# A graph layer on one core: node loads moved to GpSimd's queue, other dst blocks, a split last pair

## The chip, the core and the metric

The kernel runs on one NeuronCore of a Trainium2 chip. A core has five engines that each work through their own instruction stream: TensorE (PE, matrix multiply), VectorE (DVE), ScalarE (ACT), GpSimd (POOL) and SyncE (SP, which only issues transfers here). The metric is the device time in microseconds of one execution. The kernel before was run three times: 355.16, 357.14 and 358.20 us, so its median is 357.14 us.

## The reference, cut to what matters

There are 12,500 nodes with 128 features, and 412,500 edges with 48 features. The list `dst` names the node that each edge ends at. The inputs are sorted by it.

```python
h   = relu(layernorm(x))                                # per node, 128 features
agg = segment_sum(edge_attr, dst, num_segments=12500)   # per node, 48 features
u   = graph_globals[0]                                  # 64 numbers, the same for all nodes
hid = relu(concat([h, agg, u]) @ W1 + b1)               # 240 -> 256
out = x + hid @ W2 + b2                                 # 256 -> 128
```

Everything is float32. The edges are 79.2 MB; x and out are 6.4 MB each.

## The kernel before, in words

**Two streams of edges.** The edge list is cut into two halves, stream 0 and stream 1, which are worked in step. An edge chunk is 1024 edges, laid out as 128 partitions with 8 edges each. Six chunks of one stream make a group, and there are 34 groups per stream (`NI`). One step of the main loop (`for step in range(CG * NI + 3)`, L677) takes chunk number k of group i from both streams; I call it a k-step, and there are about 201 of them.

**The segment sum as a matrix product.** The destinations of a group fall in a narrow window of nodes. VectorE builds a one-hot matrix that says for each edge which column of the window it belongs to (`onehot`, L325 to L342: three instructions per group, for the chunk pairs 0 and 2 together and 1 alone, once the loop runs). TensorE multiplies the edges' features with it and sums in PSUM (`contract`, L344 to L357, tile `ps`). When a group is done, VectorE adds the window to the sums in SBUF at a column read from a register (`add`, L359 to L367, tile `aggT`).

**What the one-hot needs.** The list `first` holds one middle edge's dst per group, from which the window's place is taken. `dst` itself is loaded in blocks of several groups (`begins`, L79; `load_dst`, L189): a block has one row of 1024 numbers per chunk. `shift_dst` (L388) subtracts the window's place (two small matmuls, a copy, one ScalarE pass), `spread` (L400) turns the rows with eight transposes and ScalarE copies (tile `rel`), `check_dst` (L422) makes two ScalarE passes over a block that look for edges outside the window. If there were any, a slow general path would run at the end; here it doesn't.

**The node part.** Nodes are worked in pairs of blocks, one from each stream's range: 512 + 512 nodes, twelve pairs, and last a middle block of 212. For each pair: load x (`load_x`, L204; L214), statistics per row on VectorE (`bn_stats`, L491), the normalised rows on ScalarE (`xn`, L487), transposes on TensorE and a ScalarE copy out of PSUM (`transpose`, L498; tile `hT`), the first layer from x (`hidden_x`, L511; tile `ph`), the first layer from the sums (`hidden_sums`, L528), relu on ScalarE (tile `hid`), the second layer (`output`, L547; tile `po`), and an addition of x + b2 with the store (`store`, L560).

**What sets the order.** Each engine's order is fixed when the program is built. The main loop issues a k-step of `contract`, then what `plan` has for that step (loads, shifts, spreads and checks of dst blocks at fixed steps before a block begins), then at every third step an x load that is due (`next_x`), the adds and one-hots, one or two parts of the normalisation (`next_part`), and then pieces of the node part for which a credit suffices (0.72 us per step, at most 1.2; the pieces cost 0.45 or 0.9). A pair's sums may begin when the groups below its nodes are added (`ready`, L115). What is left after the last step is worked off at the end.

**Transfers.** SP issues `first`, the edge tiles (`load_edges`, L144, two chunks or 384 KB in each, 15 buffers) and the later dst blocks, and the stores. ACT's queue carries dst block 0 and all x loads, so these stand among ScalarE's compute instructions. GpSimd issues the weights once, at the start, after its constants. Transfers take one of eight completion counters in turn; the loads issued from SP and from ACT share one set of eight, those from GpSimd have another. A load that takes a counter again first waits until the counter's previous transfer has landed. The engine whose queue holds the load stops there.

**At the start**, SP issues `first` (three loads), five edge tiles, the two halves of dst block 1 (54 rows each), then the other edge tiles. ACT issues the two halves of dst block 0 (24 rows each). The blocks are 4, 9, 9, 9 and 3 groups long.

Of the kernel before, what the change touches and what calls it, by code (L numbers as in the profile page):

```python
# [9 lines left out]
F32 = mybir.dt.float32  # L10
I32 = mybir.dt.int32
AF = mybir.ActivationFunctionType
OP = mybir.AluOpType
# [3 lines left out]
P = 128  # L17
# [4 lines left out]
def kernel(  # L22
# [30 lines left out]
    nc = tc.nc  # L53
# [24 lines left out]

    begins = [0] + list(range(4, NI, 9)) + [NI]  # L79
    NB = len(begins) - 1  # L80
# [4 lines left out]
    R = 4  # L85
# [7 lines left out]

    NP = N // BN // 2
    MID = NP * BN
    NM = N - 2 * NP * BN
    END = MID + NM
    assert NM % R == 0 and NM < BN
    blocks = []
    for k in range(NP):  # L100
        blocks += [(k * BN, P), (END + k * BN, P)]
    blocks.append((MID, NM // R))
    pairs = [[2 * k, 2 * k + 1] for k in range(NP)] + [[2 * NP]]

# [10 lines left out]
    ready = [min(NI - 1, max(  # L115
        int(-(-(blocks[j][0] + BN + PAD + 1 - LEAST - BEGIN[s]) // GSTEP)) - 1
        for s, j in enumerate(pairs[k]))) for k in range(NP)]
# [78 lines left out]

    def rows_of(ap, a, m):

        return ap[a:a + m * R].rearrange("(p r) d -> p (r d)", p=m)

# [3 lines left out]
    def load_x(k):  # L204

        if k >= len(pairs):
            return
        xt = xp.tile([P, 2, R * D], F32, name="xt")
        xts[k] = xt

        def load(i, j):
            a, m = blocks[j]
            f = m - m % 16
            nc.scalar.dma_start(xt[:f, i], rows_of(x, a, f))  # L214
            if f < m:
                nc.scalar.dma_start(xt[f:m, i], rows_of(x, a + f * R, m - f))

        for i, j in enumerate(pairs[k]):
            xs[j] = xt[:, i].rearrange("p (r d) -> p r d", d=D)
            x_loads.append((k, lambda i=i, j=j: load(i, j), step))  # L220
# [19 lines left out]
    with nc.allow_non_contiguous_dma(reason="a few hundred numbers, once"):  # L240
        for s in range(2):
            mid0 = C0[s] * CE
            n = min(NI, (E - mid0) // GE)
            nc.sync.dma_start(
                first[:, s * NI:s * NI + n],
                dst[mid0:mid0 + n * GE].rearrange("(a g e) -> a g e", a=1, e=GE)[:, :, GE // 2])
            for i in range(n, NI):
                m = mid0 + i * GE + GE // 2
                assert m < E
                nc.sync.dma_start(first[:, s * NI + i:s * NI + i + 1], dst[None, m:m + 1])  # L250
    dis = {0: load_dst(0, nc.scalar)}
    for i in range(PF):
        next_edges()
        if i == 4:
            dis[1] = load_dst(1, nc.sync)

# [28 lines left out]
    eps = const.tile([P, 1], F32)  # L285
    nc.gpsimd.memset(eps, EPS)
    nc.gpsimd.memset(w1a, 0.0)
    with nc.allow_non_contiguous_dma(reason="a few hundred numbers, once"):
# [7 lines left out]
        nc.gpsimd.dma_start(b2_sb, b2[None, :].to_broadcast([P, D]))  # L296
    for c in range(0, NC, 1024):
        nc.gpsimd.memset(aggT[:, c:min(c + 1024, NC)], 0.0)
# [3 lines left out]
    nc.gpsimd.memset(span, 0.0)  # L302
    step = -4
    for k in range(XBUFS):
        load_x(k)
    warm = const.tile([P, 1], F32)
# [150 lines left out]
    def normalization(k):  # L457

        js = pairs[k]
        m = blocks[js[0]][1]  # L460
        q = len(js) * R
        st = sp.tile([P, 2 * R, 6], F32, name="st", bufs=2)
# [20 lines left out]
        def row(i, j, r):  # L483
            if r == 0:
                xns[j] = mp.tile([P, R, D], F32, name="xn")
            c = i * R + r
            nc.scalar.activation(xns[j][:m, r], xs[j][:m, r], AF.Relu, bias=sh[:m, c:c + 1], scale=sc[:m, c:c + 1])  # L487

        for i, j in enumerate(js):
            for r in range(R):  # L490
                parts.append((k, None, lambda i=i, j=j, r=r: nc.vector.bn_stats(st[:m, i * R + r, :], xs[j][:m, r, :])))  # L491
        parts.append((k, None, variance))
        parts.append((k, None, finish))
        for i, j in enumerate(js):
            for r in range(R):
                parts.append((k, j, lambda i=i, j=j, r=r: row(i, j, r)))

    def transpose(j):  # L498
        m = blocks[j][1]
        pt = pst.tile([P, R, P], F32, name="pt")  # L500
        xn = xns.pop(j)
        for r in range(R):
            nc.tensor.transpose(pt[:, r, :m], xn[:m, r], ident[:m, :m])  # L503

        hT = mp.tile([P, P, R], F32, name="hT", bufs=4)
        nc.scalar.copy(hT[:, :m], pt[:, :, :m].rearrange("d r p -> d p r"))  # L506
        hTs[j] = hT.rearrange("d p r -> d (p r)")

    phs = {}

    def hidden_x(k, a, j):  # L511

        m = blocks[j][1]
        if a == 0:
            hids[j] = mp.tile([P, NH, R, P], F32, name="hid", bufs=4)
            js = pairs[k]
            if j == js[0]:
                xb = mp.tile([P, 2 * R, D], F32, name="xb", bufs=2)
                nc.vector.tensor_tensor(xb[:m, :len(js) * R], xts[k].rearrange("p i (r d) -> p (i r) d", d=D)[:m, :len(js) * R],  # L519
                                        b2_sb[:m, None, :].to_broadcast([m, len(js) * R, D]), OP.add)  # L520
                for n, q in enumerate(js):
                    xbs[q] = xb[:, n * R:(n + 1) * R]
        phs[j, a] = psh.tile([P, BN], F32, name="ph")
        for c in (0, HI):
            nc.tensor.matmul(phs[j, a][c:c + HI, :R * m], w1h[:, a * P + c:a * P + c + HI], hTs[j][:, :R * m],  # L525
                             start=True, stop=False, skip_group_check=True)

    def hidden_sums(k, a):  # L528

        js = pairs[k]  # L530
        if len(js) == 2:
            for s, j in enumerate(js):
                at = blocks[j][0] + shift[s]
                h = slice(s * HI, s * HI + DE)
                for c in (0, HI):
                    nc.tensor.matmul(phs[j, a][c:c + HI], w1a[h, a * P + c:a * P + c + HI], aggT[h, at:at + BN],  # L536
                                     start=False, stop=True, skip_group_check=True)
        else:
            for c in (0, HI):
                nc.tensor.matmul(phs[js[0], a][c:c + HI, :NM], w1a[:K2, a * P + c:a * P + c + HI], mid[:K2],  # L540
                                 start=False, stop=True, skip_group_check=True)
        for j in js:
            m = blocks[j][1]
            nc.scalar.activation(hids[j][:, a, :, :m], phs.pop((j, a))[:, :R * m].rearrange("h (p r) -> h r p", r=R),  # L544
                                 AF.Relu, bias=bias[:, a:a + 1])

    def output(j, r):  # L547

        m = blocks[j][1]
        if r == 0:  # L550
            pos[j] = pso.tile([P, R, D], F32, name="po")
        for a in range(NH):
            for c in range(0, m, HI):
                k = min(m, c + HI)
                nc.tensor.matmul(pos[j][c:k, r], hids[j][:, a, r, c:k], w2[:, a], start=(a == 0), stop=(a == NH - 1),  # L555
                                 skip_group_check=True)
        if r == R - 1:
            late.append(j)

    def store(j):  # L560
        a0, m = blocks[j]
        ot = mp.tile([P, R, D], F32, name="ot")
        nc.vector.tensor_tensor(ot[:m], pos.pop(j)[:m], xbs.pop(j)[:m], OP.add)  # L563
        k = m - m % 16
        od = ot.rearrange("p r d -> p (r d)")
        nc.sync.dma_start(rows_of(out, a0, k), od[:k])
        if k < m:
            nc.sync.dma_start(rows_of(out, a0 + k * R, m - k), od[k:m])

# [13 lines left out]
    for k, js in enumerate(pairs):  # L583
        at = CG * ((ready + [NI - 1])[k] + 1) + 2
        nxt = pairs[k + 2] if k + 2 < len(pairs) else []
        if len(js) == 1:
            pieces.append((at, 0.0, lambda: copy_middle(0)))
        parts_of = [(at - (8 if k else 12), 0.9, lambda k=k, a=a, j=j: hidden_x(k, a, j)) for a in range(NH) for j in js]
        sums = [(at, 0.9, lambda k=k, a=a: hidden_sums(k, a)) for a in range(NH)]
        m = len(js)  # L590
        pieces += parts_of[:m + 1] + (early[2:] if k == 0 else []) + sums[:1] + parts_of[m + 1:] + sums[1:]
        for s in range(2):
            if s < len(nxt):
                pieces.append((at, 0.9, lambda j=nxt[s]: turn(j)))
            if s < len(js):
                for r in range(R):
                    pieces.append((at, 0.45, lambda j=js[s], r=r: output(j, r)))
# [46 lines left out]
    first_nodes(1)  # L644
    next_x()
    next_x()

# [29 lines left out]
    for step in range(CG * NI + 3):  # L677
# [5 lines left out]
        if step % 3 == 2:  # L683
            next_x(4)
        if k == 0:
# [12 lines left out]
        while pieces and pieces[0][0] <= step and pieces[0][1] <= credit:  # L698
            credit -= pieces[0][1]
            pop_piece()  # L700
    step += 99
    while pieces:
# [7 lines left out]
    with tc.If(isbad >= 1):  # L710
# [63 lines left out]
        for k, js in enumerate(pairs):  # L774
# [12 lines left out]
            for j in js:  # L787
                for r in range(R):
                    output(j, r)
                store_late()  # L790
# [28 lines left out]
```

## Time and profile before

| | |
|---|---|
| median of three runs | 357.14 us |
| the profiled execution: its time, and its span in the trace | 362.16 us, 360.3 us |
| TensorE busy | 310.8 us (86%) |
| VectorE, ScalarE, GpSimd busy | 239.6, 112.8, 13.9 us |
| the transfers' mean rate over the span | 265 GB/s |
| idle time of TensorE before 41.87 us | 21.6 us |
| last k-step ends, last matmul ends, span ends | 333.84, 353.06, 360.3 us |
| granted TensorE clock, mean | 0.951 |

The profile is of one execution. Each row of a view gives its start and its length in us from the span's start; `x4` counts instructions merged into one row. A float32 matmul of the program is two passes on TensorE, so a k-step is 32 instructions in the trace. A name such as `ps<-oh,e` is the tile that is written and the tiles that are read. `L351` is a line of the kernel. `SPq`, `ACTq` and `POOLq` are the issue of transfers by an engine's queue. The chain of work follows the last instruction back, at each step to what released it.

### The profile page before, as it was taken

The page shows a single profiled execution, that of the slowest core. Times are in us where ns is not written, and L with a number is a line of the kernel's source. Part 1 is how long each engine was busy: PE and PEld are TensorE (multiplying, and loading weights), DVE is VectorE, ACT ScalarE, POOL GpSimd, SP SyncE. Part 2 cuts the span into 40 slices and gives each one's busy share as a digit, 9 for nine tenths or more (in the row PEclk, how much of TensorE's full clock was granted, in tenths as well). Part 3 has the DMA queues.
Part 4 walks back from the last instruction along what each step waited for, and adds up shares of the span by engine and source line. Part 5 has one row for each costly group of instructions (what it writes and reads, how often), then busy time and mean ns, then how long its engine had stood idle before and what let it go on. Part 6 is the DMA issues. An engine that isn't in the chain of part 4 may idle for free.

```text
span 360.3 us, 17149 instructions
## 1 busy us (share of the span) xinstructions
PE 310.8 (86%) x7797; PEld 247.4 (69%) x7798; DVE 239.6 (67%) x393; ACT 112.8 (31%) x239; POOL 13.9 (4%) x51
## 2 busy tenths in 40 slices
PE   1576499899899989969969989989899999999981
PEld 1575277596588687758668678678588796886551
DVE  2958439668949658846874946977678787873420
ACT  5006343514540423340260134224253451321130
POOL 9500000000000000000000000000000000000000
PEclk9969699899899999998998989999999999999997
DMA  5999999787999986986996799998989999910111
GB/s 177 277 330 367 377 321 305 268 293 233 336 312 295 350 265 213 348 297 209 299 368 223 237 334 284 299 316 276 350 278 305 312 298 303 294 63 27 63 48 34
DMA packets 62824, 95.35 MB, mean 265 GB/s; under 512 B 4397, under 2 KB 55961, under 8 KB 62742
## 3 DMA queue, kind: packets, MB, share of 16 engines
q1 hardware_dynamic: 58852, 87.07, 73.2%
q10 hardware_dynamic: 3602, 6.60, 5.7%
q8 instruction: 63, 1.03, 1.1%
q0 software_dynamic: 288, 0.49, 0.6%
q14 instruction: 19, 0.16, 0.1%
HBM read 87.74 MB, written 6.40 MB: 261 GB/s over the span
## 4 chain that ended last, share of the span: by engine, by line
PE 73%; DMA 8%; issue 6%; DVE 5%; ACT 4%; SPq 1%; ACTq 0%; DVEq 0%
PE ps L351 37%; PE po L555 13%; PE ph L525 11%; PE ph L536 6%; DMA e<-in_edge_attr_dram 4%; PE pt L503 4%; DMA di<-in_dst_dram 3%; DVE oh L339 2%; ACT xn L487 2%; ACT hid L544 2%; PE pt L419 1%; SPq L148 1%; DVE xb L519 1%; DVE st L491 1%; DVE ot L563 0%
## 5 line engine op out<-in xcount | busy, mean ns | idle before, releaser
L351 PEld LDWEIGHTS ps<-oh,e 128*48 128x48 f32 x6448 | 177.6, 129 | 72.9 <-issue 61.7
L351 PE MATMUL ps<-oh,e 128*48 128x44 f32 (+1 forms) x6448 | 185.3, 220 | 21.5 <-issue 13.6
L339 DVE TENSOR_TENSOR oh<-iota,rel 128x1184 f32<-128x1184 f32 (+1 forms) x69 | 149.5, 2184 | 8.2 <-ACT rel L413 7.3
L555 PE MATMUL po<-w,hid 128*64 128x128 f32 (+1 forms) x784 | 61.2, 287 | 2.8 <-issue 2.0
L367 DVE TENSOR_TENSOR aggT<-aggT,ps 48x201 f32 (+1 forms) x68 | 24.4, 359 | 58.2 <-PE ps L351 36.1
L544 ACT ACTIVATE hid<-ph,bias 128x512 f32<-128x512 f32 (+1 forms) x50 | 31.1, 672 | 95.1 <-PE ph L536 91.2
L525 PE MATMUL ph<-hT,w1h 128*64 128x512 f32 (+1 forms) x200 | 52.7, 606 | 1.2 <-ACT hid L544 1.1
L555 PEld LDWEIGHTS po<-w,hid 128*64 128x64 f32 (+1 forms) x784 | 46.0, 143 | 4.4 <-issue 2.7
L487 ACT ACTIVATE xn<-xt,sh,sc 128x128 f32<-128x128 f32 (+1 forms) x100 | 40.8, 484 | 6.3 <-DMA e<-in_edge_attr_dram 4.5
L563 DVE TENSOR_TENSOR ot<-po,xb 128x512 f32<-128x512 f32 (+1 forms) x25 | 17.3, 691 | 21.7 <-PE po L555 21.3
L503 PE MATMUL pt<-ident,xn 128*128 128x128 f32 (+1 forms) x100 | 19.5, 308 | 10.8 <-ACT hT L506 6.3
L506 ACT COPY hT<-pt 128x512 f32<-128x512 f32 (+1 forms) x25 | 14.4, 574 | 45.2 <-PE pt L503 45.1
L536 PE MATMUL ph<-aggT,w1a 48*64 48x512 f32 x192 | 27.7, 632 | 0.2 <-DVE aggT L367 0.2
L491 DVE BATCH_NORM_STATS2 st<-xt 128x6 f32<-128x128 f32 (+1 forms) x100 | 22.7, 279 | 0.5 <-DMA xt<-in_x_dram 0.5
L503 PEld LDWEIGHTS pt<-ident,xn 128*128 128x128 f32 (+1 forms) x100 | 11.7, 149 | 14.4 <-ACT hT L506 6.4
L519 DVE TENSOR_TENSOR xb<-xt,b_sb 128x1024 f32<-128x1024 f32 (+1 forms) x13 | 15.2, 1172 | 0.0
L477 ACT ACTIVATE sc<-va,eps 128x8 f32<-128x8 f32 (+1 forms) x13 | 3.9, 300 | 31.4 <-DVE va L476 31.4
L525 PEld LDWEIGHTS ph<-hT,w1h 128*64 128x64 f32 x200 | 11.1, 139 | 3.8 <-ACT hid L544 2.3
L412 ACT COPY rel<-pt 128x216 f32<-128x216 f32 (+2 forms) x9 | 4.0, 444 | 26.6 <-PE pt L419 26.6
L480 DVE RECIPROCAL sc<-sc 128x8 f32<-128x8 f32 (+1 forms) x13 | 2.6, 199 | 13.3 <-ACT sc L477 13.3
L395 ACT COPY base<-pt 108x2 f32<-108x2 f32 (+2 forms) x5 | 0.8, 156 | 31.7 <-PE pt L394 31.7
L406 POOL MEMSET rel<- 128x96 f32 x1 | 0.2, 178 | 205.9 <-DVE oh L339 205.9
(84 smaller groups left out, 82.7 us busy)
## 6 DMA issues: line engine op xcount, KB each, us to landing
e<-in_edge_attr_dram SPq DMA_DIRECT2D x200, 384.0 KB
xt<-in_x_dram ACTq DMA_DIRECT2D x24, 256.0 KB
out_dram<-ot SPq DMA_DIRECT2D x24, 256.0 KB
di<-in_dst_dram SPq DMA_DIRECT2D x6, 216.0 KB
e<-in_edge_attr_dram SPq DMA_DIRECT2D x2, 192.0 KB
di<-in_dst_dram ACTq DMA_DIRECT2D x2, 96.0 KB
e<-in_edge_attr_dram SPq DMA_DIRECT2D x1, 159.0 KB
w1h<-in_L_gnn_W_dram POOLq DMA_DIRECT2D x1, 128.0 KB, 3.8
```

What stands on the lines that cost most here:

```text
L339: nc.vector.tensor_tensor(hots[i][:, at:at + n * Q * w].rearrange("p (h q w) -> p h q w", h=n, w=w), iota[:, None, None, :w].to_broadcast( ...
L351: nc.tensor.matmul(ps[s * HI:s * HI + DE, o:o + WID[k]], edges[c][0][:, t * DE:(t + 1) * DE], hot(i, s, k, t), start=(k == 0 and t == 0), ...
L367: nc.vector.tensor_tensor(to, to, acc[i % len(acc)][h, :wg], OP.add)
L487: nc.scalar.activation(xns[j][:m, r], xs[j][:m, r], AF.Relu, bias=sh[:m, c:c + 1], scale=sc[:m, c:c + 1])
L491: parts.append((k, None, lambda i=i, j=j, r=r: nc.vector.bn_stats(st[:m, i * R + r, :], xs[j][:m, r, :])))
L503: nc.tensor.transpose(pt[:, r, :m], xn[:m, r], ident[:m, :m])
L519: nc.vector.tensor_tensor(xb[:m, :len(js) * R], xts[k].rearrange("p i (r d) -> p (i r) d", d=D)[:m, :len(js) * R], b2_sb[:m, None, :].to_b ...
L525: nc.tensor.matmul(phs[j, a][c:c + HI, :R * m], w1h[:, a * P + c:a * P + c + HI], hTs[j][:, :R * m], start=True, stop=False, skip_group_ch ...
L536: nc.tensor.matmul(phs[j, a][c:c + HI], w1a[h, a * P + c:a * P + c + HI], aggT[h, at:at + BN], start=False, stop=True, skip_group_check=True)
L544: nc.scalar.activation(hids[j][:, a, :, :m], phs.pop((j, a))[:, :R * m].rearrange("h (p r) -> h r p", r=R), AF.Relu, bias=bias[:, a:a + 1])
L555: nc.tensor.matmul(pos[j][c:k, r], hids[j][:, a, r, c:k], w2[:, a], start=(a == 0), stop=(a == NH - 1), skip_group_check=True)
L563: nc.vector.tensor_tensor(ot[:m], pos.pop(j)[:m], xbs.pop(j)[:m], OP.add)
```

## The change

x and `first` are issued from GpSimd. The edge tiles come first on SP's queue. dst blocks 0 and 1 are both loaded from ACT's queue at the start, and the blocks are now 2, 6, 9, 9 and 8 groups long. GpSimd's order becomes: three loads of `first`, constants, the first two memsets of `aggT`, the two x loads of pair 0, the weights, the rest of `aggT`, and then x loads only. The x loads are queued up to three steps earlier in the program (`next_x(1)` in place of `next_x(4)`). The twelfth pair is cut into two pairs of 256 + 256 nodes; the tiles keep their size, and the instructions on these pairs take half the columns. The cost that the credit counts for a piece goes down with the block's size.

```diff
-    begins = [0] + list(range(4, NI, 9)) + [NI]
+    begins = [0, 2] + list(range(8, NI, 9)) + [NI]
...
-    NP = N // BN // 2
-    MID = NP * BN
-    NM = N - 2 * NP * BN
+    sizes = [R] * (N // BN // 2 - 1) + [2, 2]
+    NP = len(sizes)
+    MID = sum(sizes) * P
+    NM = N - 2 * MID
...
-            nc.scalar.dma_start(xt[:f, i], rows_of(x, a, f))
+            nc.gpsimd.dma_start(xt[:f, i, :r * D], rows_of(x, a, f, r))
...
-            nc.sync.dma_start(
+            nc.gpsimd.dma_start(
                 first[:, s * NI:s * NI + n],
...
-    dis = {0: load_dst(0, nc.scalar)}
+    dis = {b: load_dst(b, nc.scalar) for b in range(2)}
     for i in range(PF):
         next_edges()
-        if i == 4:
-            dis[1] = load_dst(1, nc.sync)
...
+    for c in range(0, 2048, 1024):
+        nc.gpsimd.memset(aggT[:, c:c + 1024], 0.0)
+    step = -4
+    for k in range(XBUFS):
+        load_x(k)
+    next_x()
+    next_x()
     nc.gpsimd.memset(w1a, 0.0)
...
-    for c in range(0, NC, 1024):
+    for c in range(2048, NC, 1024):
         nc.gpsimd.memset(aggT[:, c:min(c + 1024, NC)], 0.0)
...
-    step = -4
-    for k in range(XBUFS):
-        load_x(k)
...
-    next_x()
-    next_x()
...
-            next_x(4)
+            next_x(1)
...
-    step += 99
```

In `normalization`, `transpose`, `hidden_x`, `hidden_sums`, `output` and `store` the fixed 4 row sets of a block become the block's own number (4, or 2 in the last two pairs), for example:

```diff
-                    nc.tensor.matmul(phs[j, a][c:c + HI], w1a[h, a * P + c:a * P + c + HI], aggT[h, at:at + BN],
+                    nc.tensor.matmul(phs[j, a][c:c + HI, :n], w1a[h, a * P + c:a * P + c + HI], aggT[h, at:at + n],
```

## The prediction

> **What bounds the kernel now.** I read the page first: busy shares and the 40 slices (each 9 us).
>
> ```profile
> PE   1576499899899989969969989989899999999981
> PEclk9969699899899999998998989999999999999997
> ```
>
> TensorE has 8s and 9s from the sixth slice to the last but one, and is poor in the first five. From 41.87 to 333.84 us (the last k-step) it is busy 273.1 of 292.0 us; before that 20.3 of 41.9. The steady part is bound by TensorE, the start by something else. Its waits from 9 to 45 us:
>
> ```profile
> PEld pt L503 <- ACT hT L506: 6.4, 1, 6.4
> PE pt L503 <- ACT hT L506: 6.3, 1, 6.3
> PE ps L351 <- DMA e<-in_edge_attr_dram: 5.4, 3, 5.0
> ...
> ACT xn L487 <- DMA e<-in_edge_attr_dram: 4.5, 1, 4.5
> ```
>
> One wait of 6.3 us is on ScalarE, one of 5.0 on edges. The odd row is the last: `xn` reads no edges, yet ScalarE stood before it for 4.5 us because of an edge load. The chain of waits shows how:
>
> ```profile
> 29.91 8.97 DMA e<-in_edge_attr_dram
> 38.88 0.02 issue
> 38.90 0.33 ACTq L214
> 39.24 0.05 issue
> 39.29 0.88 ACT xn L487 x2
> 40.16 0.48 ACT hT L506
> 40.64 0.04 issue
> 40.69 1.25 PE pt L503 x4
> 41.94 1.11 PE ps L351 x23
> ```
>
> At 38.88 an edge load lands, and only then can ScalarE issue an x load (L214) that shares its completion counter. Normalised rows, the copy out of the one transpose buffer, the second transposes and the k-step at 41.94 follow. ScalarE was ready at 34.84, when the two passes of `check_dst` ended. In front of that, VectorE was the pace: its one-hots begin at 8.10, and its first add comes late, as the group's edges were late:
>
> ```profile
> 8.10 4.46 DVE L339 TENSOR_TENSOR oh<-iota,rel 128x1408 f32<-128x1408 f32 x3
> ...
> 23.32 0.36 DVE L367 TENSOR_TENSOR aggT<-aggT,ps 48x201 f32 x1 [2.99 <-PE ps L351]
> ```
>
> After the last k-step, the chain is TensorE and little else (19.2 us):
>
> ```profile
> 334.86 3.64 PE po L555 x64
> 338.51 2.58 PE ph L525 x12
> ...
> 345.81 3.50 PE po L555 x60
> ...
> 350.98 2.08 PE po L555 x16
> ```
>
> [...] Here `first` lands 2.3 us after its issue from SP (0.78 to 3.08), and GpSimd's weights 3.8 to 11.0 us after theirs[...]. [...] mean clock 0.88 up to 41.87 us, 0.97 after.
>
> **The change, part by part.** (1) *`first` on GpSimd.* Three issues of 0.53 to 0.74 us (as the small weight loads' rows) move GpSimd's constants 1.6 us later. The second `first` would land at about 1.3 + 3.5 = 4.8 us, against 3.97. Behind it queue the base, `df`, eight transposes, `rel`, the one-hots. ScalarE meanwhile issues four dst loads in place of two, the fourth after the first has landed (about 3.3), then its 1.28 us table load, 0.29 and 1.09 us: it is free at 6.4, where it began the base copy at 4.77 before. From base to one-hot took 8.10 - 4.77 = 3.33; smaller copies of `rel` save some 0.3. One-hots begin at 9.4, +1.3 us. Bounds: +0.2, if `first` lands as from SP, and +3.5, if it takes 7.1 as the b1 load did.
>
> (2) *Edges first, dst block 1 smaller and off their queue.* The edge tiles start at 0.78 and not 2.97, and no 432 KB of dst stands among them. What is left of the path to the first add is VectorE's own work: from 8.10 to 20.33 less 0.55 us of waiting for x, 11.7 us. 9.4 + 11.7 = 21.1, and 0.3 for the register load: 21.4 against 23.32, so -1.9. The cover is the edge supply: a group needs 6.5 tiles; by the transfers' packets the first four landed at 6.0, 7.6, 9.0 and 10.8 us, 1.6 us apart, so 6.5 take 10.4 us from about 4: 15 us. If the supply takes as long as before, this part is worth 0.
>
> (3) *dst block 1 is needed earlier.* Its shift and spread stand inside groups 0 and 1 in TensorE's order, so k-step 3 waits for a shift that follows three one-hots: 9.4 + 4.46 + 0.3 gives 14.2. The k-steps have until 21.4, and six cost at most 8.4 us at the low clock (2.79 us for two). Cost 0; without that cover some 1 to 2.
>
> (4) *x off ScalarE.* The wait from 34.84 to 39.29 goes: -4.45. The next thing on this path is ScalarE's own rows. With (2) the k-step of 41.94 begins at 35.6: -6.3 in all. GpSimd's order is short of work, so its own waits hold up nobody but x itself: pair 0's loads issue at about 6.5 and 7.2 and must be there for VectorE at 19.7; 128 KB of weights took 3.8 us, so 256 KB some 5 to 8. Pair 1's stand behind eight weight issues (4.8 us) and five memsets (3.9): about 20, landing at 26 to 30, needed at 33.2 (the row stood at 35.14). Enough, barely. The other x issues (0.33 us each) lay on an engine busy 31%: 0. The bound from the other side is the 1.6 us that two k-steps and two `ph` groups lost to the low clock after 41.9[...]. I take 0.
>
> (5) *Later dst blocks and the last block's check.* Loads, eight transposes and four copies per block are the same in number, at other steps; the last block's check now comes inside the loop, 2.7 us on ScalarE, which idles 69%: 0. VectorE's and TensorE's sums are the same.
>
> (6) *Two pairs of 256.* What is left after the last k-step, by the after-order's rows at half width: second layers 0.9 + 1.82 (three quarters of the pair before), 1.82, 1.82; first layers twice 1.33 + 0.58 + 0.45 + 0.58; transposes 0.21 + 0.33 + 0.45; the middle 0.72 + 0.39 + 2.08; that is 16.4, with waits for `hid` of about 0.5 + 0.1 + 0.5 + 0.5 + 0.6 = 2.2: 18.6 against 19.2. But 0.9 us of second layer has moved before the last k-step, and smaller matmuls add some 0.15. Net: waits 2.46 to 2.2, so about -0.1. The pace by credit, not the size of the last pair, sets how much is left. Bounds: -1 and +1.
>
> Sum: -6.3 - 0.1 = -6.4. The profiled execution (362.16, 1.8 of it outside the span) would be 355.8; it lies 5.0 above the median, and I put the same step on the median: 357.14 - 6.4 = **350.7 us**. A measurement of this kernel can tell about 1%, 3.6 us.
>
> **The rivals.** *Slower: x comes too late from GpSimd's queue* (0.12). VectorE works in order, and the statistics of pair 1 stand between two one-hots. For this: the last two weight loads took 11.0 us, and 0.49 MB of weights needed about 11.4 us (7 to 18), 43 KB/us. At that rate pair 0, the weights and pair 1 end at 20.7, 32 and 44.4: VectorE stands 11 us from 33.2, and again about 4.5 for pair 2, 15.7 in all, less the 6.4: about 366; with half of the stall beyond, 360 to 366. It decides from the point where pair 1 lands after 43. Against it: the early weight loads were far quicker.
>
> *The start's gain is taken by another wait* (0.20): `first` at its late bound, or edges still short (0 for part 2), so that 1 to 3 us remain: 355. Speaking for it: the start has several waits of like size behind one another.
>
> *More than the start* (0.15): 13.6 us of the steady part are TensorE waits put down to "issue", often in the middle of a k-step, and followed by the low clock. If a part of these came from ScalarE's and SP's shared counters, 3 to 5 us more: 346. Against it: they start at no buffer's boundary.
>
> **How the numbers follow.** Forecast case 0.53: 350.7, of its own 347.5 to 353.5. To leave out no more than 2 in 10, I go from 345 (the lower half of the big-gain case and below left out) to 358.5 (the slower case left out). Faster by over 1% (below 353.6): 0.50 of the forecast case and 0.15, 0.65. Within 1%: 0.03 and 0.19, 0.22. Slower: 0.13.
>
> **What would show it.** In the profile after: no ScalarE row before an `xn` that waits for an edge load; first one-hot near 9.4, first add near 21.4; the k-step behind the second transposes near 35.6; the time from the last k-step to the last matmul within 1 us of 19.2. A VectorE statistics row (`st`) that waits for x for several us before 60 us would make the forecast wrong, and so would a first k-step group that still waits for edges after 20 us.

## The result, and the profile after

| | before | after |
|---|---|---|
| median, 20 runs of each | 356.89 us | 353.78 us |
| ratio, with its 95% interval | | 0.9855 (0.9816 to 0.9893) |
| profiled execution: time, span | 362.16, 360.3 us | 351.11, 349.3 us |
| profiled once more: time, span | 354.73, 352.9 us | 350.01, 347.8 us |

The change makes the kernel 1.45% faster, about 5.2 us of 356.89. The medians of all 20 runs of each give 0.991, 3.1 us; ratios here are formed only from those runs of a kernel that lie within 1.5% of its fastest (16 of before, 10 of after). The forecast was 6.4 us off a median of 357.14. The first profile of before was 5 us above its kernel's median. Of the 11 us between the first two profiles, half is therefore not the change, and I use the second pair beside the first.

The busy shares and the clock of after, in 40 slices of 8.7 us:

```profile
PE   0697977999999799989999989998998999999981
PEclk9996988999999999999999999999999999999997
```

In before the first five slices were 1, 5, 7, 6, 4. Here the first two are 0 and 6, and from the third on TensorE has a 7 or more up to the last; the 7s are the fourth, sixth and seventh slice (up to 61 us) and the fourteenth. Here are some of the waits of TensorE and ScalarE in after from 9 to 45 us (engine and tile, what they waited for, total, times, longest):

```profile
PE pt L456 <- issue: 2.7, 1, 2.7
...
PE ps L356 <- DVE oh L344: 2.3, 1, 2.3
...
ACT xn L492 <- DVE sh L486: 0.9, 2, 0.5
```

ScalarE's 4.5 us for an edge load ahead of `xn` are gone, and so are TensorE's 5.0 us for edges. What is left in front of `xn` is VectorE's own statistics. In all the waits of these 36 us there is no `st` row that waits for x. TensorE's longest wait, 2.7 us up to 28.75, has no named cause ("issue"); before has none of over 0.7 us there. The chain runs over VectorE at that time, so it does not set the 15th k-step. It is of the kind that "What these waits are" below describes. The chain of waits of after:

```profile
1.31 0.68 POOL first L247
1.99 5.75 DMA first<-in_dst_dram
...
11.51 4.46 DVE oh L344 x3
...
23.40 0.34 DVE aggT L372
...
34.90 0.77 ACT xn L492 x2
...
37.30 0.84 PE ps L356 x32
```

`first` took 5.75 us from its issue on GpSimd. Because of that the one-hots begin at 11.51 (8.10 before) and the first add lies at 23.40, where it lay at 23.32. But the k-step behind the second transposes begins at 37.30 in place of 41.94: 4.64 us earlier. Then the chain shows a wait that before did not have here:

```profile
46.25 2.00 issue
48.25 2.25 PE ps L356 x61
...
53.42 2.21 issue
55.63 2.86 PE ps L356 x34
```

Two times within a k-step TensorE stands for 2 us and waits for nothing that the profile names. The end is as it was: the last k-step ends at 322.52 and the last matmul at 341.82, 19.3 us later (19.2 before). The lines that answer to those shown of before:

```profile
330.08 1.93 PE po L562 x32
...
339.75 2.08 PE po L562 x16
```

To see where the time went I read four marks from each trace: the first add, the begin of the 15th k-step (in before and after the one behind the second transposes), of the 27th and of the 61st. They are read from the rows of TensorE themselves, which begin 0.07 us ahead of the chain's. "Waits" are the TensorE waits of over 0.7 us that name no cause, between the 15th and 27th.

| | first add | 15th | waits | 27th | 61st | ratio |
|---|---|---|---|---|---|---|
| before | 23.3 | 41.9 | none | 58.3 | 114.5 | 1 |
| before, second profile | 23.5 | 43.0 | 1.0 | 60.5 | 114.7 | |
| after | 23.4 | 37.2 | 2.0 + 2.2 | 56.9 | 108.7 | 0.9855 |
| after, second profile | 23.3 | 37.1 | 3.5 | 55.6 | 107.2 | |

At the 61st k-step after is 5.9 us ahead in the first profiles and 7.5 in the second. From there to the last k-step's end the two executions of before took 219.3 and 211.8 us, those of after 213.9 and 214.0. In these four profiles the gain is made in the first 110 us; behind that, the two executions of before differ by more than the kernels do. That difference of 7.6 us is for the most part unnamed waits of over 0.7 us (9.3 and 4.8 us in this stretch) and TensorE's busy time (205.2 and 201.7 us, at a granted clock of 0.977 and 1.000). In the first 110 us the gain is made by the 15th k-step (4.6 and 5.9 us), shrinks to 1.4 and 4.9 at the 27th, where after has its unnamed waits, and comes back until the 61st.

### The profile page after: what moved, and what is told of

Its sections match the earlier page's. It is cut to its first block, busy times and chain, and to the rows that moved or that the text cites. A ratio compares the mean times of both kernels' runs of the same rounds, so it can differ in the third digit from the quotient of the medians.

```text
span 349.3 us, 17266 instructions
## 1 busy us (share of the span) xinstructions
PE 307.3 (88%) x7829; PEld 247.0 (71%) x7830; DVE 240.4 (69%) x403; ACT 116.7 (33%) x250; POOL 30.4 (9%) x82
## 4 chain that ended last, share of the span: by engine, by line
PE 79%; DVE 8%; issue 5%; ACT 4%; DMA 2%; DVEq 0%; POOL 0%; ACTq 0%; POOLq 0%
PE ps L356 41%; PE po L562 13%; PE ph L531 12%; PE ph L543 7%; DVE oh L344 5%; PE pt L508 4%; DMA first<-in_dst_dram 2%; PE pt L424 1%; ACT xn L492 1%; ACT hid L551 1%; ACT far L432 1%; DVE st L496 1%; DVE aggT L372 0%; DVE ot L570 0%; DVE brow L380 0%
## 5 line engine op out<-in xcount | busy, mean ns | idle before, releaser
L356 PE MATMUL ps<-oh,e 128*48 128x44 f32 (+1 forms) x6448 | 187.2, 220 | 18.1 <-issue 15.6
L551 ACT ACTIVATE hid<-ph,bias 128x512 f32<-128x512 f32 (+2 forms) x54 | 32.0, 643 | 90.9 <-PE ph L543 88.4
L531 PE MATMUL ph<-hT,w1h 128*64 128x512 f32 (+2 forms) x216 | 52.6, 565 | 1.2 <-ACT hid L551 1.2
L217 POOL DMA_DIRECT2D xt<-in_x_dram x27 | 14.5, 540 | 257.7 <-issue 257.7
L570 DVE TENSOR_TENSOR ot<-po,xb 128x512 f32<-128x512 f32 (+2 forms) x27 | 17.6, 651 | 21.4 <-PE po L562 20.6
L512 ACT COPY hT<-pt 128x512 f32<-128x512 f32 (+2 forms) x27 | 14.7, 543 | 47.8 <-PE pt L508 47.8
L543 PE MATMUL ph<-aggT,w1a 48*64 48x512 f32 (+1 forms) x208 | 27.3, 587 | 0.8 <-DVE aggT L372 0.8
L482 ACT ACTIVATE sc<-va,eps 128x8 f32<-128x8 f32 (+2 forms) x14 | 4.2, 299 | 49.1 <-DVE va L481 49.1
L525 DVE TENSOR_TENSOR xb<-xt,b_sb 128x1024 f32<-128x1024 f32 (+2 forms) x14 | 15.4, 1098 | 0.1
L417 ACT COPY rel<-pt 128x216 f32<-128x216 f32 (+3 forms) x9 | 4.1, 451 | 14.3 <-PE pt L424 14.3
L543 PEld LDWEIGHTS ph<-aggT,w1a 48*64 48x64 f32 x208 | 5.7, 134 | 3.8 <-issue 2.4
```

Of the source, the lines that this page charges most:

```text
L356: nc.tensor.matmul(ps[s * HI:s * HI + DE, o:o + WID[k]], edges[c][0][:, t * DE:(t + 1) * DE], hot(i, s, k, t), start=(k == 0 and t == 0), ...
L525: nc.vector.tensor_tensor(xb[:m, :n, :nr], xts[k].rearrange("p i (r d) -> p i r d", d=D)[:m, :n, :nr], b2_sb[:m, None, None, :].to_broadca ...
L531: nc.tensor.matmul(phs[j, a][c:c + HI, :nr * m], w1h[:, a * P + c:a * P + c + HI], hTs[j], start=True, stop=False, skip_group_check=True)
L543: nc.tensor.matmul(phs[j, a][c:c + HI, :n], w1a[h, a * P + c:a * P + c + HI], aggT[h, at:at + n], start=False, stop=True, skip_group_check ...
L551: nc.scalar.activation(hids[j][:, a, :nr, :m], phs.pop((j, a))[:, :nr * m].rearrange("h (p r) -> h r p", r=nr), AF.Relu, bias=bias[:, a:a ...
L570: nc.vector.tensor_tensor(ot[:m, :nr], pos.pop(j)[:m, :nr], xbs.pop(j)[:m, :nr], OP.add)
```

## The experiments

The theories at the start of the tests were those of the prediction: the gain is ScalarE's wait for an edge load, which goes because x leaves its queue; `first` from GpSimd takes away what the earlier edges bring. The rivals were that the dst blocks and the order of the edges make the gain, and that something else sets the pace once the start is shorter. Each experiment has its marks in one table at the end of this section.

**`first` from SP again.** In after, the three loads of `first` go back to SP, ahead of the edges; all else stays.

```diff
-            nc.gpsimd.dma_start(
+            nc.sync.dma_start(
                 first[:, s * NI + i:s * NI + n],
```

> The changed kernel with the three loads of the middle edges' dst (first) back on SP's queue, ahead of the edge tiles; all else as changed. Theory (the gain is ScalarE's wait for an edge load, gone with the x loads; the late landing of first took back what the earlier edges could bring): the second row of brow at about 4.0 us and not 7.8, first one-hot at 9.5 and not 11.5 (ScalarE is then held by its four dst loads), first add at 21.4 and not 23.4, the k-step behind the second transposes at 35.3 and not 37.3; in time 2 us below the changed kernel, 351 to 352. Rival (the gain is that edges come first): the edge tiles start 2.2 us later, so the time rises by about 2 us to 356.

Ratio 0.9855 (0.9807 to 0.9904), the same as after's. `first` came 3.0 us sooner (4.73), yet the one-hots began only 0.8 us sooner (10.72). ScalarE was now the late one. Its waits from 0 to 45 us and the chain:

```profile
ACT base L400 <- PE pt L399: 6.0, 1, 6.0
...
ACT L312 <- DMA first<-in_dst_dram: 4.9, 1, 4.9
```

```profile
1.63 3.10 DMA first<-in_dst_dram
...
4.74 0.30 ACTq L180
...
50.73 4.59 issue
```

ScalarE's fourth dst load takes a counter that `first` holds when both come from SP and ACT. It goes out at 4.74; the table load (1.28 us), the base and `df` follow it. Later an unnamed wait of 4.59 us takes the rest: the 15th k-step is 0.8 us earlier than in after, the 27th only 0.3.

**x from GpSimd, nothing else.** In before, only the two x loads change their queue.

```diff
-            nc.scalar.dma_start(xt[:f, i], rows_of(x, a, f))
+            nc.gpsimd.dma_start(xt[:f, i], rows_of(x, a, f))
```

> The kernel before with one edit: x is loaded from GpSimd's queue. Theory: one-hots begin at 8.1 and the first add comes at 23.3 as before, no xn waits for an edge load, the k-step behind the second transposes begins at about 37.5 and not 41.9; in time 4.4 us below before, 352.5. Rival (the gain is the edges' place and the dst blocks, or the halved last pairs): within 1 us of before, 357.

Ratio 0.9959 (0.9922 to 0.9996): 0.4%, less than a third of the whole change. ScalarE's wait for edges ahead of `xn` is gone, as the prediction has it. TensorE's waits for edges are longer in its place, 9.6 us where before had 5.4, and VectorE waits 4.0 us for x (waits from 5 to 45 us, then the chain):

```profile
PE ps L351 <- DMA e<-in_edge_attr_dram: 9.6, 5, 4.8
...
DVE st L491 <- DMA xt<-in_x_dram: 4.0, 1, 4.0
```

```profile
10.10 17.37 DMA e<-in_edge_attr_dram
...
27.60 4.06 PE ps L351 x96
```

GpSimd issues all eight x loads of the first four pairs in a burst, from 13.8 to 19.3 us. By the transfers' packets its queue (x and 0.49 MB of weights) had moved 0.68 MB at 20 us and 2.59 MB at 28. In these 8 us 3.3 edge tiles landed, in before 5.4, where ACT's queue moved 0.4 MB of x: 1.5 MB more of x in these 8 us went with 2.1 fewer edge tiles of 384 KB. In after six x loads go out in a burst as well, from 19.0 to 21.9, and from 24 to 28 us only 1.3 tiles landed. But there 14.2 tiles were in by 24 us, in this kernel 9.0, and TensorE didn't run out of them.

**The same, with x held back.** In the kernel of the last experiment, GpSimd copies one number of `st` ahead of the x loads of the third and fourth pair, so that these go out only when VectorE is at that statistic.

```diff
+            held = {2: (0, 7), 3: (1, 0)}.get(k)
+            if held and held[0] in sts and k not in came:
+                nc.gpsimd.tensor_copy(dummy, sts[held[0]][0:1, held[1], 0:1])
```

> The kernel before with x on GpSimd's queue (as e2), and the x loads of pairs 2 and 3 held back by a one-number copy on GpSimd that reads statistics of pairs 0 and 1. Theory (in e2, eight x loads issued at once took 1.9 MB between 20 and 28 us, only 3.3 edge tiles landed in that time, and TensorE waited for edges): 4 tiles or more land from 20 to 28 us, the wait for edges shrinks from 9.6 us to below 5, the 15th k-step begins at 38 and not 41.3, time 353, 2 us below e2. Rival (the x move alone is worth no more, whatever the edges do): 355, as e2.

Ratio 0.9895 (0.9846 to 0.9945). From 20 to 28 us 5.8 edge tiles landed in place of 3.3, and TensorE waited 1.5 us for edges in place of 9.6. The first add is back at 23.2 and the 15th k-step begins at 37.0, as in after, with none of the change's other parts. So the mechanism of part 4 is real: with x off ScalarE, and not in the edges' way, the kernel before has after's start. In time the two kernels are less clearly apart than in these marks: the intervals of 0.9959 and 0.9895 just overlap.

**Everything but x.** In after, x goes back to ScalarE's queue, at its old places.

```diff
-            nc.gpsimd.dma_start(xt[:f, i, :r * D], rows_of(x, a, f, r))
+            nc.scalar.dma_start(xt[:f, i, :r * D], rows_of(x, a, f, r))
...
-            next_x(1)
+            next_x(4)
```

> The changed kernel with x back on ScalarE's queue, at its old places in the program; all else as changed. Theory: ScalarE stands before an xn for an edge load again, the k-step behind the second transposes comes 4 to 5 us later than 37.3, and the time is 358, slightly above before, as first still lands late. Rival (edges first and the small dst block are the gain): 354, as changed.

Ratio 0.9872 (0.984 to 0.9904): nearly the whole gain without the move of x. ScalarE's wait for an edge load is still there, 4.4 us long, but at another place (waits from 5 to 45 us, and the chain):

```profile
ACT rel L415 <- DMA e<-in_edge_attr_dram: 4.4, 1, 4.4
```

```profile
11.32 12.04 DMA e<-in_edge_attr_dram
...
23.38 0.34 ACTq L217
...
23.76 0.40 ACT rel L415
```

It ends at 23.36, ahead of `rel` of dst block 1, where VectorE still has its adds to do. The 15th k-step begins at 38.9, 1.7 us behind after's.

**The dst blocks alone.** In before: the blocks of 2, 6, 9, 9 and 8 groups, blocks 0 and 1 both from ACT at the start, so that no dst stands among SP's edges. x stays on ScalarE, `first` on SP ahead of the edges, the last pair whole.

```diff
-    begins = [0] + list(range(4, NI, 9)) + [NI]
+    begins = [0, 2] + list(range(8, NI, 9)) + [NI]
...
-    dis = {0: load_dst(0, nc.scalar)}
+    dis = {b: load_dst(b, nc.scalar) for b in range(2)}
...
-        if i == 4:
-            dis[1] = load_dst(1, nc.sync)
```

> The kernel before with one part of the change: dst blocks of 2, 6, 9, 9, 8 groups, blocks 0 and 1 both from ScalarE's queue, so that no dst stands among the edge tiles on SP; x stays on ScalarE's queue, first on SP, the pairs as before. Theory now (the start was short of edges, because 432 KB of dst stood in front of them, and ScalarE's wait for an edge load was a part of that): the first add no longer waits 3 us for TensorE, the k-step behind the second transposes (the 15th) begins at 37 to 39 and not 41.9, time 352.5, as low as with x on ScalarE and all the rest changed (e4). Rival (first on GpSimd or the x loads are needed for the gain): within 1 us of before, 356.

Ratio 0.9856 (0.9819 to 0.9893): the whole gain, from parts 2 and 3 alone. ScalarE still waits ahead of `xn`, for 3.0 us where it was 4.5, and the 15th k-step begins at 39.8. 10.1 tiles had landed at 20 us in place of 7.6, and the edge load that holds ScalarE's counter lands at 36.85 and not at 38.88. That is 2.0 us at this mark; how it becomes the ratio's 5.1 us one profile does not show. The size of the blocks and their queue were not tried apart.

**A shorter start.** In after: `first` on SP, dst block 1 back on SP behind five edge tiles, and block 0's check two groups later.

```diff
-    dis = {b: load_dst(b, nc.scalar) for b in range(2)}
+    dis = {0: load_dst(0, nc.scalar)}
...
+        if i == 4:
+            dis[1] = load_dst(1, nc.sync)
...
-        at_step(begins[b] + (3 if b else 1), 5, lambda b=b: check_dst(b, dfs[b]))
+        at_step(begins[b] + 3, 5, lambda b=b: check_dst(b, dfs[b]))
```

> The changed kernel with first on SP's queue ahead of the edges, dst block 1 on SP's queue behind five edge tiles, and the two ScalarE passes of check_dst on block 0 moved from step 11 to step 23. Theory: ScalarE and first are both early, one-hots begin at about 8.0 and not 11.5, the first add at 20 and not 23.4, the 15th k-step at 32 and not 37.2, since the passes of check_dst (2.4 us) no longer stand between two sets of xn; a part of these 5 us is given back by the 27th k-step[...]; time 350.5. Rival (edges are short again with dst and first in front of them): the first add stays at 23, time 354 or more.

Ratio 0.983 (0.977 to 0.989), not to be told from after's. The first one-hot is at 7.5 and the 15th k-step at 35.7, the earliest of all. The profiled execution took 362.23 us, 11 us more than this kernel's median, so its marks carry less weight. Three unnamed waits between the 15th and the 27th take the lead back:

```profile
45.73 2.00 issue
...
49.87 1.56 PE ps L358 x63
51.43 4.59 issue
56.02 2.86 PE ps L358 x34
```

**What these waits are.** I counted TensorE's instructions (matmuls, weight loads and the few others on its stream, such as semaphore waits) up to each unnamed wait of over 0.7 us. Behind the 15th k-step there are eight in after, and all come where the count, divided by 256, leaves 193, the first two at 1473 and 1729. In before there are seven, in the other profiles four to twelve, and every one leaves 193. So does the wait of 2.7 us that ends at 28.75 in after. One queue of the page carries pieces that fit:

```profile
q8 instruction: 63, 1.03, 1.2%
```

These are 63 packets of 16,384 bytes. The trace of after has 15,753 instructions of TensorE, which is 61.5 times 256: at 256 to a packet, an estimate from these counts, they need 62 packets, and 63 came. In after a packet began at 45.6 and took 1.1 us, and TensorE went on at 48.25. The next began at 52.9 and took 1.1 us, and TensorE went on at 55.63. Over all the profiles TensorE goes on 1.2 to 1.7 us after the packet's end. From these counts and times I read that TensorE waits here for its own instructions; no row of the profile names it. Up to 46 us the packets of after begin 6.5 us apart (19.5, 26.2, 32.7, 39.2, 45.6), while TensorE needs less for 256 instructions. From the 1473rd to the 1729th it took 3.7 us at full clock without the wait (second profile of after, 47.12 to 54.34 less 3.49), and 5.2 in the first profile, where the clock was half for 3.4 us of it. In before the packets began 6.3 to 6.8 us apart too (18.1, 24.9, 31.3, 37.6) while TensorE stood 6.3 us for ScalarE, so they do not keep to TensorE's pace, and before has no unnamed wait of over 0.7 us until 62.5. Two experiments change the edges' loads, to see whether the packets come closer together.

**Ten edge buffers.** In after, the edges have 10 buffers and not 15.

```diff
-    PF = 15
+    PF = 10
```

> The changed kernel with 10 edge buffers in place of 15. Theory (TensorE's waits put down to issue all stand at the same place in a 256-instruction block and end 1.3 to 1.6 us after a 16 KB fetch of instructions[...]): the buffers are full some 10 us earlier, the waits of 2.0 and 2.2 us at 46 and 53 us fall below 1 us each, the 27th k-step begins at 54 and not 56.9, time 2 to 3 us below the changed kernel, 351. Rival (the buffers' depth covers waits for edges): TensorE waits for edges more often, 355 to 358; or the two waits stay, 354.

Ratio 0.9884 (0.9849 to 0.9919): no gain over after. The 27th came at 54.4, about as the theory had it, but an unnamed wait of 2.7 us stayed, where after has 4.2 or 3.5, and the time did not follow. With either number of buffers the loads from SP take eight counters in turn (eight in the trace of after), so that no more than eight can be out at a time.

**Half tiles.** In after, an edge tile is one chunk (192 KB), and there are 30 of them. The eight counters then hold half as many bytes.

```diff
-    CL = 2
-    PF = 15
+    CL = 1
+    PF = 30
```

> The changed kernel with edge tiles of one chunk (192 KB) in place of two, and 30 buffers in place of 15: the same bytes in the same order, but at most half as many edge bytes asked for at a time, as an issue waits for the eighth load before it. Theory (TensorE's waits put down to issue are waits for 16 KB blocks of its own instructions, and a block takes 6.5 us while eight edge loads of 384 KB are outstanding): in the first 55 us the blocks come 4 to 5 us apart, the two waits of 2.0 and 2.2 us at 46 and 53 us fall below 1 us each, the 27th k-step begins at 53 to 54 and not 56.9; time 350 or less. Rival (a block's time does not hang on the outstanding edge bytes): blocks 6.5 us apart, the two waits stay; time 354 or, with 400 issues in place of 200, more.

Ratio 0.9667 (0.9591 to 0.9742), the fastest version of this study, median 342.41. The edges came no faster: 10.7 tiles' worth at 20 us and 18.0 at 32, in after 10.9 and 18.7. The packets of instructions begin 5.7 us apart on average, from 18.5 to 47.0 us; in the second profile of after it is 6.2. The chain after the 15th k-step:

```profile
48.58 0.88 issue
49.47 1.67 PE ps L356 x64
...
54.41 2.08 issue
```

From the 15th to the 27th k-step this kernel took 13.8 us and after 19.7. Of the 5.9 between, 3.3 are unnamed waits. The other 2.6 are TensorE's own work: it was busy 12.9 us at a granted clock of 1.00, in after 15.4 us at 0.88. In after two stretches of 3.4 us at half clock begin at 48.8 and 55.6; the waits of 2.0 and 2.2 us end at 48.25 and 55.63. Between the ratios 0.9855 and 0.9667 lie 6.7 us of 356.89. This kernel leads after by 6.7 us at the 27th k-step. The wait of 2.08 us at 54.41 and slower rows behind it (eight instructions of `ph` in 1.79 us, ahead of the wait in 1.02) make it 4.1 at the 61st, and at the last k-step it is 6.4 (322.5 and 316.1). Against the second profile of after the three are 5.4, 2.6 and 5.1. So the gain in time is measured, and a part of it is fewer waits at the start; where the rest lies one profile does not show.

**Half tiles in the kernel before.** Is that a gain of its own? The same in before, with dst block 1 behind the same bytes of edges.

```diff
-    CL = 2
-    PF = 15
+    CL = 1
+    PF = 30
...
-        if i == 4:
+        if i == 9:
```

> The kernel before with edge tiles of one chunk (192 KB) in 30 buffers, the dst block 1 still behind the same 1.92 MB of edges; nothing of the change. Theory[...]: blocks at the start come 5 to 6 us apart where they were 6.5, and the ratio to the kernel before is 0.975 to 0.985, that is, the half tiles are worth 5 to 9 us on either kernel. Rival (the halves are worth something only once the change has taken the x loads off the counters that the edges share): ratio 0.99 to 1.01, ScalarE still waits for an edge load ahead of the normalised rows, and with twice as many loads per counter perhaps longer.

Ratio 0.9967 (0.9929 to 1.0004): nothing that can be measured. The rival is right. With x on ScalarE, its loads share eight counters with twice as many edge loads (waits from 20 to 60 us):

```profile
PE pt L503 <- ACT hT L506: 8.6, 1, 8.6
ACT xn L487 <- DMA e<-in_edge_attr_dram: 7.8, 1, 7.8
```

4.5 us have become 7.8, ahead of the same `xn`. The 15th k-step begins at 46.7, and no unnamed wait of over 0.7 us follows up to the 27th. Behind the 15th k-step its unnamed waits add up to 4.7 us (12.9 and 9.5 in the profiles of before), but what was lost ahead of it is not won back. So smaller loads pay only together with the change. That it is x on ScalarE's queue that stands in their way is what the wait of 7.8 us says; half tiles with x alone moved were not tried.

**The last pair whole.** In after, the twelfth pair stays 512 + 512.

```diff
-    sizes = [R] * (N // BN // 2 - 1) + [2, 2]
+    sizes = [R] * (N // BN // 2)
```

> The changed kernel with twelve pairs of 512 + 512 nodes, as before, and all else as changed. Theory (the halved pairs bring nothing, the pace by credit sets what is left at the end): 353.8, within 1.5 us, and about 19 us from the last k-step to the last matmul. Rival (a smaller last pair shortens the end): 3 us above the changed kernel, 357, with the end longer by as much.

Ratio 0.9879 (0.982 to 0.9939), not to be told from 0.9855; from the last k-step to the last matmul 19.2 us. Part 6 is worth nothing that can be measured.

**Both kernels again.** One more profile of before and of after, unchanged, on one chip.

> The kernel before, unchanged, for a second profile. Theory: 14 to 15 tiles of the edges have landed at 30 us, the 15th k-step begins at 41 to 42, the 27th at 58 to 59 us as in the first profile; the stretch from there to the last k-step, 275.5 us in the first profile, differs by some us, since that profile lay 5 us above the median: 270 to 272.

> The changed kernel, unchanged, for a second profile. Theory: first one-hot at 11.5, first add at 23.4, 15th k-step at 37.2, waits of about 2 us at 46 and 53 us, 27th k-step at 57 us, as in the first profile; from there to the last k-step 266 to 269 us.

Their rows stand in the table of marks in the section on the result. They show what a single profile is worth: the marks up to the 15th k-step repeat within 1.1 us, the 27th within 2.2, and the stretch behind the 61st within 7.5.

All marks, in the order of the 15th k-step:

| edit | first add | 15th | waits | 27th | 61st | ratio, interval |
|---|---|---|---|---|---|---|
| half tiles in before | 22.2 | 46.7 | none | 63.1 | 116.0 | 0.9967 (0.9929 to 1.0004) |
| x alone | 26.7 | 41.3 | 1.7 | 58.0 | 109.5 | 0.9959 (0.9922 to 0.9996) |
| dst blocks alone | 22.7 | 39.8 | 3.5 | 58.6 | 110.9 | 0.9856 (0.9819 to 0.9893) |
| everything but x | 23.5 | 38.9 | 3.5 | 57.3 | 112.7 | 0.9872 (0.984 to 0.9904) |
| ten buffers | 23.3 | 37.1 | 2.7 | 54.4 | 107.8 | 0.9884 (0.9849 to 0.9919) |
| last pair whole | 23.2 | 37.0 | 4.0 | 55.7 | 106.9 | 0.9879 (0.982 to 0.9939) |
| x alone, held | 23.2 | 37.0 | 3.7 | 56.7 | 111.9 | 0.9895 (0.9846 to 0.9945) |
| `first` from SP | 22.6 | 36.4 | 6.5 | 56.6 | 108.9 | 0.9855 (0.9807 to 0.9904) |
| half tiles in after | 22.6 | 36.4 | 0.9 | 50.2 | 104.6 | 0.9667 (0.9591 to 0.9742) |
| shorter start | 21.8 | 35.7 | 7.8 | 57.3 | 111.7 | 0.983 (0.977 to 0.989) |

With whole tiles the 15th k-step moves by 5.6 us from x alone to the shorter start, and the 27th lies between 54.4 and 58.6 with no order in it: mostly, the earlier the 15th, the longer the waits. That fits what the ratios show, that the edits don't add, though with one profile of each kernel it isn't shown as their cause. The 61st k-step does not follow the ratios either: x alone is early there (109.5) and gains least. A profile is of one execution, and some lie well off their kernel's median (everything but x 5.7 us above, the dst blocks alone 4.0 below). Either x held back or the dst blocks alone give most of the change's gain, and the whole change gives no more.

## Why the prediction was right or wrong

The sum was near (6.4 us forecast, 5.2 by the ratio), and the reason given for its main term holds only in part. That it was so near is partly luck: 1.9 us of it did not come, and how the lead at the 15th k-step turns into the gain at the end was not foreseen.

1. *`first` on GpSimd, +1.3.* Mis-sized. The second `first` landed at 7.74, not at 4.8; the one-hots began at 11.51, not 9.4. That is +3.4, the late bound of +3.5. I had taken 3.5 us for a load from GpSimd, and this one took 5.75. But the first experiment shows that this cost nothing in time: from SP, ScalarE's fourth dst load waits for the same counter and is ready at 7.66 and not at the 6.4 of my sum.
2. *Edges first, the first add at 21.4.* The working was right, its start was not: from the first one-hot to the first add I had 12.0 us, and it took 11.9. With the late one-hots the add stayed at 23.4, and the 1.9 us at this mark were lost. The edge supply carried it: 10.9 tiles had landed at 20 us, 7.6 before, and TensorE's wait of 5.0 us for edges is gone.
3. *dst block 1 earlier, 0.* Right: no wait for it is on the chain of after.
4. *x off ScalarE, -4.45.* The wait is gone and the k-step came at 37.30: 4.64 of the 6.3 us that I had with part 2. The step "the wait from 34.84 to 39.29 goes" was right, and x held back shows that moving x can do it. As an account of the gain it was incomplete. The wait was for an edge load that landed late. The dst blocks alone, which let the edges land sooner, bring 1.44% with x still on ScalarE; x alone brings 0.4%, and 1.05% when it is held out of the edges' way. My sum counted parts 2 and 4 as two gains in a row. By the ratios they are two ways to one gain, and what the sum left out of part 4 is the price of the burst.

   *The clock and the time after, at the end of part 4, 0.* I took it that TensorE keeps its pace from the earlier k-step on. It stood 4.2 us in two of the unnamed waits before the 27th. Its clock was 0.88 from the 15th to the 27th, hardly another than before's 0.90. The waits are the rival "the start's gain is taken by another wait", which I had looked for in `first` and the edges. It took 3.2 of the 4.6 us at this mark in the first pair of profiles and 1.1 of 5.9 in the second; by the 61st k-step after was ahead by more than at the 15th, since before meets such waits too, only later (1.79 us at 62.5).
5. *Later dst blocks and the last block's check, 0.* Right: behind 35 us the chain of after has no ScalarE or VectorE row of a dst block and no wait for one, only TensorE's own transposes and small matmuls for it.
6. *Two pairs of 256, -0.1.* Right: 19.3 against 19.2, and the whole pair tells no difference.

The rival with x too late fell: no statistic of after waits for x. It was near, though, in the kernel with x alone (4.0 us for x, and 9.6 for the edges behind it): in after pair 0's x is issued ahead of the weights, and more edges have landed before the next x loads go out; which of the two spares it wasn't tried. The rival with more than the start had the right place, the waits put down to "issue", and the wrong cause: their positions follow the count of TensorE's instructions (193 over a multiple of 256) and not the counters of ScalarE and SP, and there are about as many after (eight of over 0.7 us, 12.3 us, behind the 15th k-step) as before (seven, 12.9 us).

Left open: why the packets of instructions begin 6.2 to 6.5 us apart at the start of after. With smaller loads in flight it was 5.7 us. That they wait behind the edges' loads is not shown by this: half tiles change other things too, the grain at which TensorE's edges arrive among them. And the 61st k-step's time scatters by 5.8 us between kernels of ratios 0.987 and 0.988; one profile of each can't tell what of that is theirs.

## What to carry to other kernels

A wait that the profile puts on a counter or a queue can have two cures: take the waiter off that queue, or make the thing in front of it finish sooner. Cost them as alternatives, not as a sum, and ask what in the same stage is next within a few us. When loads move to a queue that has nothing else to wait for, they can go out in a burst ahead of what is needed first, as with x alone (1.9 MB of x in 8 us, and 3.3 edge tiles where before had 5.4); then hold them back (5.8 tiles). And if TensorE stops in mid-tile with no named cause, count its instructions: here every such wait of over 0.7 us lay at 193 over a multiple of 256, and that pointed to their supply.

## What was not expected of the hardware

- TensorE stopped at like places of its instruction count. Every unnamed wait of over 0.7 us lay at 193 over a multiple of 256 and ended 1.2 to 1.7 us after a packet of 16,384 bytes on the queue that the page calls `instruction`, and single waits were up to 4.6 us long. At the start, with up to eight loads of 384 KB in flight, packets began 6.5 and 6.2 us apart in the two profiles of after; with 192 KB 5.7.
- The three loads of `first`, of at most 34 numbers, took 4.8 to 7.0 us from issue to landing on GpSimd's queue in after, where the first of them took 2.3 from SP in before. The time is not fixed: with half tiles the same three loads took 3.3 to 3.6 us.
- The one-hots on VectorE ran at the same 3,091 ns in both kernels, although GpSimd is now busy for 30.4 us and not 13.9. Of the 16.5 us more, 14.5 are the issue of x loads, so this says little about other work on GpSimd.
